# Bias, centring, causal mask and residual moved between TensorE and VectorE, with a new order, in a Mamba and MoE block

## The chip, the cores and the metric

The kernel runs on one core of one Trainium2 chip. The time is the device time of one execution in microseconds. The core has five engines with instruction queues of their own, each in order: TensorE (PE in the profile, with its weight loads as PEld), VectorE (DVE), ScalarE (ACT), GpSimd (POOL) and SyncE (SP), which here only issues DMAs.

## The reference

The input x is 4 x 1024 tokens of 128 numbers, all float32. Two blocks follow each other, each with a residual and a layer norm. First a Mamba block:

```python
xz = x @ in_proj.T; xb, z = split(xz)            # 256 channels each
xb = silu(conv4(xb)); dt = softplus(...); B, C = ...
h[t] = exp(dt*A) * h[t-1] + dt*xb*B              # 16 states a channel
y = (h * C).sum(states) + xb * D_param
y = layernorm(y) * silu(z); x = layernorm(x + y @ out_w.T)
```

Then a transformer block with 16 heads of 8 numbers, causal softmax attention, and a mixture of 16 experts (128 to 512 to 128, gelu), each token going to its best two within a capacity of 512 slots an expert:

```python
q, k, v = layernorm(x) @ q_w, ...                # scores only where key <= query
hidden = x + (softmax(q k / sqrt(8)) v) @ o_w + o_b
xt = layernorm(hidden); top1, top2 = best two of xt @ router_w
out = layernorm(x + hidden + gates * experts(xt))
```

## The kernel before

The tokens are cut into nine units: seven of 512 tokens (0 to 6) and two of 256 (7 and 8, the end of batch 3). A unit passes through these stages, whose names carry its number:

- `conv` and `dt`: the projection, convolution and step sizes, written to DRAM.
- `scan`: the recurrence. A page holds 32 channels x 4 states; VectorE multiplies (`uB`), scans (L527) and multiplies again (`hC`), ScalarE makes the decay (`da`), TensorE sums over the states (`py`).
- `norm`: y is centred by two products with a fixed matrix (`centre`), squared, averaged over channels by 128x1 products (`pvar`), and the inverse root `rs` comes from a power on GpSimd (`inv_power`, L501 on POOL). Then the output projection (`pa`, `pbx`), the residual x by a product with the identity, two layer norms (`affine`), `x1` and `xn`.
- `qk`: queries and keys, each split into three bf16 parts (`part`) that go to DRAM (`parts`) and come back as the operands of the scores.
- `att`: for four groups of four heads, blocks of 128 keys: `scores`, on diagonal blocks a bf16 product of the identity with a mask added into the same bank, the exponential (`pr`) and the average (`av`) on TensorE; at a group's end `avs`, `av_tr`, `rc`, `ctx`.
- `post`: output projection with its bias, which is a product of a row of ones with a row `obp`; layer norm; the row buffer `xrow`, of which there are three, with the token's number copied into its last column by GpSimd (`tokcol`); the router's logits.
- `route`: for chunks of units (0,1), (2,3), (4,5), (6), (7), (8), the two best experts, their slots, and per 128 tokens two indirect sends from `xrow` on GpSimd (L2151).

After them the experts make two passes over 16 experts, the first over slots 0 to 127 and 384 to 511, the second over the middle, each ending in indirect scatters on GpSimd (L2300). `finish` loads the two expert rows of a token (`got`), weights and adds them, on VectorE (L521) or with diagonal matrices on TensorE, normalises and stores.

Nothing of this runs in program order. Each operation is declared with a value `v`, its possible engines and an estimated duration, and a planner (`Plan.schedule`) then simulates the engines: whenever one is free, it takes the ready operation with the lowest `v`. A table `ORDER` adds an offset to `v` by stage and by name of the operation. An operation's `v` is never below that of what it depends on. The planner's result is written out as the fixed order of each engine's queue. The planner does not know the real times: a wrong estimate makes an engine wait in front of an operation that it thinks is ready.

Lines of helpers: L451 matmul, L449 transpose, L479 and L474 ScalarE, L481 to L487 the same work given to VectorE, L501 tensor_tensor, L512 and L514 tensor_scalar, L521 scalar_tensor_tensor, L527 scan, L428 DMAs.

Of the kernel before, what the change touches and what calls it, by code (L numbers as in the profile page):

```python
# [9 lines left out]
F32 = mybir.dt.float32  # L10
# [8 lines left out]
P = 128  # L19
# [41 lines left out]
    "att0": 38, "att1": 41, "att2": 38, "att3": 8.5, "att4": 25, "att5": 9.5, "att6": 22, "att7": 43, "att8": 117,  # L61
    "conv1": 8, "conv2": 22, "conv3": 55, "conv4": -4, "conv6": 8, "conv7": 12, "dt3": 90, "dt5": 43, "fc1": 8,
    "norm0": 45, "norm1": -25, "norm2": -52, "norm3": 5, "norm5": -3, "norm6": -48, "norm7": -26.5, "norm8": 15,
    "place2": 75, "post0": -112, "post1": 3, "post2": 79, "post3": 32, "post4": -87, "post5": 30, "post6": -23,
    "post7": 12, "qk4": 52, "qk6": 22, "qk7": 27, "route0": -107, "route1": -328, "route3": 58, "scan0": 7,
    "scan1": 36, "scan2": 30, "scan3": 26, "scan4": 37.5, "scan5": 22.5, "scan6": 15, "scan7": -1.5, "scan8": 45.5,
    "x1": 160, "av_tr": -308, "avs": -104, "b1_tr": 43, "centre": -78, "constants": -38, "conv": 56.9, "ctx": -74,
    "ctx_tr": 21.5, "dt": 27, "dt_sp": 48, "dtmm": 29, "fin": 72, "first": -9, "flags": 54, "got": 153, "kst": -25,
    "lg": 65, "ln2_ag": 49, "m_t": 49, "part": 7, "pbias": 62, "pqk": 3, "pr": -356, "pv": 16.12, "rc": -135,
    "rest": 132, "rs": 34, "scan": 10, "scores": -2.05, "sz_s": 36, "t_first": 17, "token": 185, "u": 34,  # L70
    "u_sp": 58, "w_out_b": 115, "wide": 71, "x2_tr": 61.5, "xT": 53, "xT0": 49, "x_rows": 39.4, "xe_tr": 4,
    "xnT": 52,
# [115 lines left out]
class Plan:  # L188
    def __init__(self, nc, tc, loaded=None, order=()):
# [57 lines left out]
    def schedule(self):  # L247
# [77 lines left out]
        while n_left:  # L325
# [8 lines left out]
            while again:  # L334
                again = False
                for e in engines:
# [55 lines left out]
                    if op.wire:  # L392
                        bus = max(bus, op.end) + op.wire
                        op.done = bus + (2300 if e == "POOL" else 1500)
# [22 lines left out]
class Emit:  # L417
# [80 lines left out]
    def tt(self, v, out, a, b, op, pool=False, name=""):  # L498
        eng = self.nc.gpsimd if pool else self.nc.vector
        fixed = 250 + 420 * out.cols if op == ALU.pow else None  # L500
# [74 lines left out]
def mamba_then_moe_block_kernel(ctx: ExitStack, tc: tile.TileContext, a: dict, out: bass.AP):  # L575
# [866 lines left out]
    plan_a = Plan(nc, tc)  # L1442
# [193 lines left out]
    def mild_path(ph):  # L1636
        DVE_FROM = 6
# [28 lines left out]
        }  # L1666
        conv_half, dt_half, adopt = fronts_of(p, e, 3)
# [181 lines left out]
        def inv_power(v, pool_name, src, n, two, name):  # L1849
# [3 lines left out]
            if two:  # L1853
                e.ts(v, ve[:, 1, :], src, 1.0 + LN_EPS, LN_EPS * LN_EPS, ALU.mult, ALU.add, name=name)
# [616 lines left out]
```

## Time and profile before

| | |
|---|---|
| median of 6 runs | 1019.6 us (1015.96 to 1024.89) |
| profiled execution | 1019.58 us, span 1017.7 us |
| granted TensorE clock, mean | 0.948 |
| TensorE busy | 872.8 us, 86% |
| VectorE busy | 800.0 us, 79% |
| ScalarE busy | 717.5 us, 71% |
| GpSimd busy | 243.9 us, 24% |
| DMA | 166.14 MB, 163 GB/s on average |

The shares are averages over stages with different limits, so they say little by themselves. The scans end at 735 us; by then unit 7's attention is under way. From there to the end at 1017.7 us come the attention of units 7 and 8, the two expert passes and `finish`. A chain of waits is read backwards from the last instruction: each piece is what released the next.

### The profile page before, as it was taken

The page shows a single profiled execution, that of the slowest core. Times are in us where ns is not written, and L with a number is a line of the kernel's source. Part 1 is how long each engine was busy: PE and PEld are TensorE (multiplying, and loading weights), DVE is VectorE, ACT ScalarE, POOL GpSimd, SP SyncE. Part 2 cuts the span into 40 slices and gives each one's busy share as a digit, 9 for nine tenths or more (in the row PEclk, how much of TensorE's full clock was granted, in tenths as well). Part 3 has the DMA queues.
Part 4 walks back from the last instruction along what each step waited for, and adds up shares of the span by engine and source line. Part 5 has one row for each costly group of instructions (what it writes and reads, how often), then busy time and mean ns, then how long its engine had stood idle before and what let it go on. Part 6 is the DMA issues. An engine that isn't in the chain of part 4 may idle for free.

```text
span 1017.7 us, 17751 instructions
## 1 busy us (share of the span) xinstructions
PE 872.8 (86%) x6309; PEld 471.9 (46%) x6351; DVE 800.0 (79%) x1488; ACT 717.5 (71%) x1152; POOL 243.9 (24%) x340
## 2 busy tenths in 40 slices
PE   7878989779986999998989989988983889997983
PEld 3323344234442345444335443434562448887963
DVE  3999999999999999999989989997952233434234
ACT  3667878649975997997988889886852666453321
POOL 2000000420010001068010110182016133554541
PEclk9999989799988999999998999999996999999997
DMA  4767965887644555575383545263892324215233
GB/s 123 236 222 226 341 230 196 287 251 211 184 126 135 180 148 154 157 227 151 102 263 111 166 116 172 80 186 86 268 259 78 104 69 122 66 58 156 64 115 105
DMA packets 143437, 166.14 MB, mean 163 GB/s; under 512 B 15521, under 2 KB 97764, under 8 KB 143204
## 3 DMA queue, kind: packets, MB, share of 16 engines
q1 hardware_dynamic: 138084, 156.07, 50.4%
q0 software_dynamic: 4096, 8.43, 2.5%
q8 instruction: 54, 0.88, 0.4%
q10 hardware_dynamic: 1152, 0.34, 0.1%
q14 instruction: 51, 0.42, 0.1%
HBM read 108.10 MB, written 56.69 MB: 162 GB/s over the span
## 4 chain that ended last, share of the span: by engine, by line
PE 37%; DVE 25%; DMA 11%; ACT 9%; issue 7%; POOL 6%; another core or an unknown queue 2%; SPq 2%; DVEq 0%; ACTq 0%; POOLq 0%
PE bank L451 21%; PE pair L451 13%; DVE arena L527 11%; DVE arena L501 10%; ACT arena L479 8%; POOL xin L2151 4%; PE bank L449 2%; DMA xin<-rt_full 2%; DVE arena L521 2%; SPq L428 2%; DMA xin<-xrow,rt_put 1%; DMA arena<-q_parts 1%; DMA arena<-eout 1%; DMA arena<-k_parts 1%
## 5 line engine op out<-in xcount | busy, mean ns | idle before, releaser
L479 ACT ACTIVATE arena<-pair 128x1024 f32<-128x1024 f32 (+2 forms) x341 | 302.4, 924 | 58.0 <-PE pair L451 32.7
L501 DVE TENSOR_TENSOR arena<-arena 128x2048 f32<-128x2048 f32 (+2 forms) x154 | 303.1, 1985 | 0.4 <-PE bank L451 0.3
L451 PE MATMUL pair<-arena 128*128 128x256 bf16 (+4 forms) x1079 | 250.0, 329 | 43.3 <-ACT arena L479 22.9
L479 ACT ACTIVATE arena<-arena,f_a_neg 128x512 f32<-128x512 f32 (+1 forms) x284 | 183.7, 680 | 60.1 <-DVE arena L527 48.9
L501 POOL TENSOR_TENSOR smalls<-smalls,neg_half 128x4 f32<-128x4 f32 (+2 forms) x35 | 61.5, 1758 | 514.0 <-DVE smalls L512 351.3
L451 PE MATMUL bank<-arena,vp 128*32 128x256 f32 (+3 forms) x1728 | 166.9, 469 | 3.9 <-ACT arena L474 1.2
L527 DVE TENSOR_TENSOR_SCAN arena<-arena,state 128x512 f32<-128x512 f32 (+1 forms) x160 | 162.1, 1050 | 0.0
L451 PEld LDWEIGHTS <-arena 128*128 128x128 bf16 x864 | 81.0, 99 | 157.1 <-issue 120.9
L527 DVE TENSOR_TENSOR_SCAN arena<-arena 128x512 f32<-128x512 f32 x128 | 150.1, 1204 | 0.0
L2151 POOL DMA_INDIRECT xin<-xrow,rt_put x64 | 88.8, 1388 | 92.2 <-ACT arena L479 30.0
L479 ACT ACTIVATE arena<-pair,b 128x256 f32<-128x256 f32 x128 | 53.6, 471 | 59.7 <-PE pair L451 54.2
L451 PE MATMUL pair<-mask_k,identb 128*128 128x128 bf16 x512 | 94.0, 222 | 1.3 <-issue 0.4
L451 PE MATMUL bank<-arena,f_sel 128*32 128x512 f32 x512 | 71.3, 631 | 19.9 <-DVE arena L501 19.7
L2300 POOL DMA_INDIRECT eout<-arena,to x64 | 62.4, 975 | 55.0 <-DVE arena L501 29.5
L451 PEld LDWEIGHTS bank<-arena,vp 128*32 128x32 f32 x1728 | 38.3, 110 | 63.2 <-issue 42.8
L501 DVE TENSOR_TENSOR arena<-bank,arena 128x256 f32<-128x256 f32 (+2 forms) x46 | 22.0, 479 | 57.7 <-PE bank L451 52.0
L451 PEld LDWEIGHTS bank<-arena 128*128 128x128 f32 x512 | 63.6, 196 | 3.2 <-DVE arena L501 1.2
L451 PE MATMUL bank<-arena 128*128 128x128 f32 x512 | 64.2, 280 | 0.8 <-DVE arena L501 0.8
L451 PEld LDWEIGHTS <-identb 128*128 128x128 bf16 x512 | 50.7, 99 | 9.3 <-issue 7.7
L451 PEld LDWEIGHTS pair<-arena 128*128 128x128 f32 x256 | 44.8, 194 | 13.2 <-ACT arena L479 9.2
L449 PE MATMUL bank<-ident,arena 128*128 128x128 f32 (+1 forms) x257 | 45.3, 289 | 5.3 <-ACT arena L474 2.0
L479 ACT ACTIVATE arena<-arena,smalls 128x128 f32<-128x128 f32 x59 | 26.1, 497 | 30.9 <-DVE smalls L521 30.9
(216 smaller groups left out, 1070.3 us busy)
## 6 DMA issues: line engine op xcount, KB each, us to landing
arena<-k_parts SPq DMA_DIRECT2D x52, 288.0 KB
arena<-bc_h SPq DMA_DIRECT2D x56, 256.0 KB
arena<-dt_h SPq DMA_DIRECT2D x52, 256.0 KB
arena<-u_h SPq DMA_DIRECT2D x52, 256.0 KB
arena<-in_fc_w_dram SPq DMA_DIRECT2D x32, 256.0 KB
q_parts<-halves SPq DMA_DIRECT2D x21, 384.0 KB
k_parts<-halves SPq DMA_DIRECT2D x21, 384.0 KB
arena<-q_parts SPq DMA_DIRECT2D x28, 288.0 KB
```

What stands on the lines that cost most here:

```text
L428: return self.p.add(v, {queue: 460}, lambda e: engine.dma_start(out.real(), in_.real()), [out], [in_], name, wire=wire, after=after)
L449: nc.tensor.transpose(out.real(), lhsT.real(), rhs.real())
L451: nc.tensor.matmul(out.real(), lhsT=lhsT.real(), rhs=rhs.real(), start=bool(start), stop=stop, skip_group_check=start is None)
L479: nc.scalar.activation(out.real(), in_.real(), func, scale=real(scale), **kw)
L501: return self._dve(v, lambda e: eng.tensor_tensor(out.real(), a.real(), b.real(), op), [out], [a, b], out.cols, fixed=fixed, name=name, po ...
L521: return self._dve(v, lambda e: nc.vector.scalar_tensor_tensor(out.real(), a.real(), real(s), b.real(), op0, op1), [out], self._views(a, s ...
L527: return self._dve(v, lambda e: nc.vector.tensor_tensor_scan(out.real(), d0.real(), d1.real(), real(init), ALU.mult, ALU.add), [out], self ...
L2151: inst = nc.gpsimd.indirect_dma_start(out=dst.real()[:, :], out_offset=bass.IndirectOffsetOnAxis(ap=idx.real(), axis=0), in_=src.real(), i ...
L2300: inst = nc.gpsimd.indirect_dma_start(out=eo_d.real()[:, :], out_offset=bass.IndirectOffsetOnAxis(ap=idx.real(), axis=0), in_=src.real(), ...
```

## The change

The functions and constants that change:

- Units 7 and 8 (`u >= MASK_FROM`): no mask product; VectorE multiplies the exponential's diagonal 128x128 blocks of four heads at once by a triangle of ones and zeros (`below`). Their centring is one mean from TensorE (two products) and two additions on VectorE (`apart`).
- The output bias: `obp` is a 128x128 bf16 tile of zeros with the bias, split in three bf16 parts, in rows 0, 32 and 64; it is multiplied by a bf16 tile of ones.
- `pvar`: products with a 128x32 tile into four row groups, a copy `var`, a transpose `pvar_t`.
- Units 6 to 8: the residual x is added by VectorE instead of an identity product.
- `inv_power` and `affine`: the double power is two powers, the second half's first, and so are the products `nm`.
- `tokcol` is placed behind the power and `nm` of its post stage.
- The planner: landing of a GpSimd DMA 3500 ns instead of 2300, a power 80 + 310 ns a column instead of 250 + 420, a send 1450 and a scatter 1320 instead of 1260, loads ahead of the branch 1.5 times as long with a landing of 3000.
- `finish`: blocks 12, 20 and 28 by TensorE instead of 16, 20, 24 and 28.
- Every entry of `ORDER` is new.

```diff
 ORDER = {
-    "att0": 38, "att1": 41, "att2": 38, "att3": 8.5, "att4": 25, "att5": 9.5, "att6": 22, "att7": 43, "att8": 117,
...
+    "att0": -22, "att1": 30, "att2": 43, "att3": 7, "att4": 15, "att5": -0.5, "att6": 29, "att7": 32, "att8": 125,
...
+    "qk1": -175, "qk4": 32, "route1": 37, "route2": -8, "route3": -8, "route5": 49, "scan0": -12, "scan1": -8.5,
+    "scan2": 28, "scan3": 3, "scan4": 10.2, "scan6": -4, "scan7": 21, "scan8": 37.5, "top2": 105, "x1": 154,
+    "x2": 105.5, "av": 23, "av_tr": 26.9, "b1_tr": 4, "before": 45, "below": 90, "bt": 31, "constants": -5,
...
 }
...
-                        bus = max(bus, op.end) + op.wire
-                        op.done = bus + (2300 if e == "POOL" else 1500)
+                        bus = max(bus, op.end) + op.wire * self.wire
+                        op.done = bus + (3500 if e == "POOL" else self.landing)
...
-        fixed = 250 + 420 * out.cols if op == ALU.pow else None
+        fixed = 80 + 310 * out.cols if op == ALU.pow else None
...
-    plan_a = Plan(nc, tc)
+    plan_a = Plan(nc, tc, wire=1.5, landing=3000)
...
-            e.pe(v + 5, [("mm", pb[0:1, 0:D], fx(vbc), fx(wo), True, True)], name="pbias")
-            e.tt(v + 5, fx(obp), ob, pb[0:1, 0:D], ALU.add, name="obp")
+            wide = new("tmp", "vb_wide")[:, 0:P]
+            e.copy(v + 4, wide, fx(vbc).to_broadcast([P, P]), name="obp")
+            e.pe(v + 5, [("mm", pb[:, 0:D], wide, fx(wo), True, True)], name="pbias")
+            e.tt(v + 5, ob, ob, pb[:, 0:D], ALU.add, name="obp")
+            part = wide.bitcast(BF16)[:, 0:D]
+            for i in range(3):
+                e.copy(v + 5, part, ob, name="obp")
+                e.copy(v + 5, fx(obp)[32 * i : 32 * i + 1, :], part[32 * i : 32 * i + 1, :], name="obp")
+                if i < 2:
+                    e.tt(v + 5, ob, ob, part, ALU.subtract, name="obp")
...
-            e.tt(v, r.rearrange("p k n -> p (k n)"), ve.rearrange("p k n -> p (k n)"), fx(neg_half)[:, 0 : k * n], ALU.pow, pool=True, name=name + "_pow")
...
+            for i in reversed(range(k)):
+                e.tt(v, r[:, i, :], ve[:, i, :], fx(neg_half)[:, 0:n], ALU.pow, pool=True, name=name + "_pow")
...
+            if u >= MASK_FROM:
+                mean = new("bank", "centred")[:, 0:n]
+                e.pe(v, [("mm", mean, fx(center)[:, 1, :], y[c], c == 0, c == NC2 - 1) for c in range(NC2)], name="centre")
             for c in range(NC2):
-                pt = new("bank", "centred")[:, 0:n]
-                e.pe(v, [("mm", pt, fx(center)[:, 0, :], y[c], True, False), ("mm", pt, fx(center)[:, 1, :], y[1 - c], False, True)], name="centre")
+                if u >= MASK_FROM:
+                    pt = new("tmp", "apart")[:, 0:n]
+                    e.tt(v + 0.5, pt, y[c], mean, ALU.add, name="apart")
+                else:
...
-            e.pe(v + 2, [("mm", pv[:, i : i + 1], sqs[c][:, tok(i)], fx(mean_col), c == 0, c == NC2 - 1) for i in range(nt) for c in range(NC2)], name="pvar")
+            pv = new("bank", "pvar")[:, 0:P]
+            e.pe(v + 2, [("mm", pv[32 * i : 32 * i + 32, :], fx(mean_w), sqs[c][:, tok(i)], c == 0, c == NC2 - 1) for c in range(NC2) for i in range(nt)], share=3.4, name="pvar")
+            var = new("var")[:, 0:P]
+            e.act(v + 2, var[0 : 32 * nt, :], pv[0 : 32 * nt, :], AF.Copy, dve=u >= DVE_FROM, name="var")
+            pv = new("bank", "pvar_t")[:, 0:P]
+            e.pe(v + 2, [("tr", pv[:, 0 : 32 * nt], var[0 : 32 * nt, :], fx(ident)[0 : 32 * nt, 0 : 32 * nt], 0, 0)], name="pvar_t")
+            pv = pv[:, 0 : 32 * nt : 32]
...
+            if u >= DVE_FROM:
+                e.tt(v + 4.5, xp, xp, r, ALU.add, name="xp")
...
-                            if diag:
+                            if masked:
                                 calls.append(("mm", pst[:, jj, :P], fx(identb), fx(mask_k), False, True))
...
+                        if diag and u >= MASK_FROM:
+                            e.tt(vv + 0.1 * j0 + dv * 0.6, pr[:, 0:per, 0:P], pr[:, 0:per, 0:P], fx(tri).unsqueeze(1).to_broadcast([P, per, P]), ALU.mult, name="below")
...
-            e.copy(v, xrow[:, :, D], fx(token)[:, tile0 : tile0 + nt], pool=True, name="tokcol")
+            p.behind(e.copy(v, xrow[:, :, D], fx(token)[:, tile0 : tile0 + nt], pool=True, name="tokcol"), [rr_op])
...
-        by_pe = range(2 * TPB, NT, 4)
+        by_pe = (12, 20, 28)
```

## The prediction

> **What bounds the kernel now.** I read the slices of the span first, to see which engine is full when; then a table of stages that I cut at the places where that changes; then the chain of waits inside the two stages where nothing is full; then the groups, for prices. Busy tenths of three engines in 40 slices of 25.4 us:
>
> ```profile
> PE   7878989779986999998989989988983889997983
> DVE  3999999999999999999989989997952233434234
> PEclk9999989799988999999998999999996999999997
> ```
>
> VectorE is full for some 28 slices, then TensorE for the rest, with a hole at slices 30 and 31. The stages (PE, weight loads, VectorE, ScalarE, GpSimd in us, then granted clock, DMA share, GB/s):
>
> ```profile
> 50.00:735.00 685.00, 603.63 (x4302) 277.14 (x4345) 662.98 (x887) 560.56 (x864) 121.11 (x96) 0.96 0.59 184
> 768.00:788.00 20.00, 5.36 (x40) 2.24 (x39) 0.95 (x8) 2.71 (x6) 14.73 (x29) 0.62 0.31 94
> 788.00:843.00 55.00, 48.12 (x531) 27.27 (x532) 14.91 (x104) 37.01 (x46) 13.31 (x25) 0.95 0.30 86
> 932.00:938.00 6.00, 0.71 (x5) 0.40 (x4) 3.01 (x15) 1.15 (x4) 5.26 (x9) 0.90 0.22 67
> 938.00:982.00 44.00, 44.00 (x279) 39.80 (x280) 11.42 (x33) 17.58 (x43) 26.75 (x50) 0.94 0.21 63
> 982.00:1017.70 35.70, 14.35 (x131) 10.80 (x129) 17.50 (x89) 4.41 (x11) 6.46 (x7) 0.77 0.49 140
> ```
>
> To 735 us VectorE (scans) has 22.0 us idle in 685. After that nothing new comes from the scans, and TensorE should run through; it does not in 768 to 788 (14.6 us idle) and 932 to 938 (5.3 us idle). What the chain says there, and at 687 to 696 where ScalarE starved (start, us, what):
>
> ```profile
> 686.60 5.14 DMA xin<-xrow,rt_put
> 691.89 1.29 POOL xrow L540
> 693.18 2.75 POOL smalls L501
> 695.95 0.63 ACT arena L479 x2
> ...
> 767.62 3.58 another core or an unknown queue
> 772.52 5.16 another core or an unknown queue
> 778.18 4.45 another core or an unknown queue
> 782.75 5.66 another core or an unknown queue
> ```
>
> The first is a queue effect: GpSimd's token copy waits 4.07 us for a send that still reads its buffer, and the power that unit 7's `rs` needs stands behind it. The second has no named releaser. In it GpSimd alone works, on the 16 sends of units 4 and 5, one every 1.26 us from 765.4, while ScalarE moves unit 8's query and key parts in steps of about 5 us. Prices (the last column before the bar is the count, after it busy us and mean ns):
>
> ```profile
> L451 PE MATMUL pair<-mask_k,identb 128*128 128x128 bf16 x512 | 94.0, 222 | 1.3 <-issue 0.4
> L501 DVE TENSOR_TENSOR arena<-arena 128x512 f32<-128x512 f32 x23 | 15.4, 675 | 0.1
> L451 PE MATMUL bank<-obp,ones_row 1*128 1x512 f32 x14 | 7.8, 640 | 0.1
> L501 POOL TENSOR_TENSOR smalls<-smalls,neg_half 128x8 f32<-128x8 f32 x7 | 17.5, 2504 | 100.7 <-DVE smalls L514 79.6 <-DVE smalls L512 21.1
> L501 POOL TENSOR_TENSOR smalls<-smalls,neg_half 128x4 f32<-128x4 f32 x24 | 39.1, 1628 | 394.6 <-DVE smalls L512 311.9 <-DVE rt_full L501 40.7 <-DVE flags L512 30.3
> ```
>
> **The sum's base** is the profiled execution: 1019.6 us, of which 1017.7 is span; the median of the runs is the same 1019.6.
>
> **The change part by part.** *Mask.* 64 of the 512 mask products go (units 7 and 8: 4 groups x 2 diagonal blocks x 4 heads each). They are pipelined: at 826 us a score and its mask take 0.17 us from start to start, a score alone 0.11, so each saves 0.055, 3.5 us of TensorE. VectorE gets 16 multiplies of 128x512, 16 x 0.68 = 10.8 us, in 768 to 843, where it is a quarter busy. Each stands between the exponential and the average, whose next scores are already out; uncovered only at a group's end, 8 x 0.7 = 5.6 us. Queued behind a multiply that waits for its exponential are VectorE's copies of finished averages and the routing of units 6 and 7; VectorE's 40 free us of 55 there take that up. Between -3.5 and +2; I take -3, since TensorE has other scores to run.
>
> *Bias.* The f32 row product (1.12 us a pair) becomes one bf16 product; the 128x512 bf16 row with neg_identb takes 0.39. 0.7 us a unit; only units 6 to 8 lie behind the scans: -1 (0 to -2). The new constants are some nine small VectorE instructions of 0.23 (the cast of a 128x128 at 21 us): +2, inside VectorE's full stage. The bias is now loaded into 128 rows, 64 KB instead of 512 bytes, still one issue on SP's queue in the first 60 us; the 128 KB load of `center` beside it is of the same kind: 0.
>
> *Centring, units 7 and 8.* TensorE loses half of 2.08 us for both; VectorE gains 4 x 0.42 (128x256 from PSUM), 0.84 of it in the full stage. *Residual, units 6 to 8.* TensorE loses 1.2 + 0.6 + 0.6; VectorE gains 0.68 + 2 x 0.42, of it 1.1 in the full stage; TensorE's part after 735 counts -1.
>
> *Variance.* Sixteen short products (1.0 us) become sixteen in four row groups (0.43 for eight, as the averages with vp), a copy (0.37 ScalarE, 0.27 VectorE) and a transpose (0.31). TensorE gains nothing to speak of, the chain to `rs` gets 0.7 longer. VectorE's other work hides it in units 0 to 7; unit 8: +0.7.
>
> *Powers.* One 128x8 of 2.50 us becomes two 128x4 of 1.63, the wanted one first: `xn` starts 0.9 earlier, `x1` 0.8 later, GpSimd works 0.76 more a unit. Hidden by the scans, in units 7 and 8 about -0.5. The doubled `nm` adds 0.15 to VectorE in seven units before 735: +1.
>
> *Token copy* goes behind the post stage's power. The 4.07 wait no longer holds `rs`; what is late next is ScalarE's turn on the exponentials: -3 (0 to -4).
>
> VectorE's full stage thus grows by 2 + 0.84 + 1.1 + 1 = 5 us; its 22 idle could swallow it (0), but full slices lie close together, so +5.
>
> *Last sums.* One more block of eight on VectorE (8 x 0.28 = 2.2), one less on TensorE (about 2.4 by 16 x 0.15). Both wait for the same loads: -1 (-3 to +2).
>
> *Order.* All offsets are new, so are a send's landing (3500 for 2300) and the price of a power and a send, and the planner moves everything: loads on SP's queue, sends and powers on GpSimd's. Which instruction stands where I can't read from the offsets. From below its gain ends at the idle time: 14.6 + 5.3 + 22.0, about 42 us. From above it can make as big a hole as the 20 us of 768 to 788 a second time. I take 10 of the first hole, as sends are now held to land later so that work behind them is planned apart, 3 of the second (the scatters and the first `got` loads are also re-placed) and nothing of VectorE's: -13. The first branch's own new prices for loads touch the 50 us before the scans fill VectorE: 0 (-3 to +3).
>
> Sum: -3 -1 -1 +0.7 -0.5 -3 +5 -1 -13 = -16.8, so 1003.
>
> **A rule against it.** Row: unit 7's 128x2 power at 693.1 took 2.78 us while VectorE ran two 128x2048 multiplies for 4.48; the twice as wide power at 935.6, with VectorE nearly idle, took 1.04. The Trainium skill, SBUF — State Buffer, Who interferes with whom, says that a VectorE instruction with two SBUF inputs locks out a GpSimd one that reads SBUF, for its whole length. The new multiplies are of that kind. By the rule each could hold up a power or send, 16 x 0.68 = 11 us of GpSimd at worst, and the sum would be near 1014. The sum above sets 0: GpSimd has 42 us free in 788 to 843.
>
> **Rivals.** *(a) The hole closes.* If 768 to 788 is only the meeting of 16 sends with unit 8's parts, another order ends it: all 14.6 and 5.3 go, and 5 of VectorE's idle: local terms -3.8, order -25: 991. For it: GpSimd is the only busy engine there. Against: no releaser is named, so the order may not reach it.
>
> *(b) The order moves nothing.* Only the local terms remain: 1019.6 - 3.8 = 1016. For it: VectorE and TensorE are at 97% and near 100% in their stages. Against: two holes and a starved power that are queue effects.
>
> *(c) Slower.* GpSimd's sends come in front of unit 8's power. Place: after the scans' end, 735 to 768, where unit 8 runs centre to query product in 28 us with GpSimd 5.7 busy in 33. If 16 sends of 1.26 stand ahead of its two powers, its attention starts up to 20 later; the old hole can't hide this, for then TensorE has only unit 7. It decides from seven sends on: 8.8 us less the local 3.8 is the 5 that can be told. Price 20 - 4 = +16: 1035; with half, 1026. For it: the sends come in batches of 16 already, and routing's place moves by tens of units. Against: a send's price is raised, which pulls powers ahead.
>
> **How the numbers follow.** Forecast 0.40, (a) 0.24, (b) 0.14, (c) 0.22. What can be told from no change is 0.5%, 5 us. Faster: forecast, (a) and a fifth of (b), 0.67; same: the rest of (b), 0.11; slower: (c), 0.22. The range: (a) with 12 more of VectorE's idle used, 979, to half of (c) and its spread, 1030. The forecast with (a) alone would span 979 to 1014.
>
> **What would show it.** mask_k rows 448 instead of 512, sixteen more 128x512 VectorE products, no 128x8 power, an obp product in bf16, and no token copy between a landing send and a power. The stage of full VectorE should end at 735 to 742. The forecast is wrong if TensorE still idles over 10 us in one piece after 760, if the hole has moved rather than closed, or if VectorE's stage ends after 750.

## The result, and the profile after

The changed kernel takes 1028.88 us (median of 20 runs, 1020.72 to 1034.78) where the kernel before takes 1018.25 in runs beside it (46 runs, 1013.4 to 1027.13). The ratio on record, which is not the quotient of the two medians (that would be 1.0104), is 1.0086, with a 95% interval of 1.0065 to 1.0107: slower by 0.86%. The forecast was 1003, with 979 to 1030 as its range. The profiled execution took 1026.14 us, with a span of 1024.3 and a mean granted clock of 0.947 (before: 1019.58, 1017.7, 0.948).

The slices of the changed kernel, busy tenths in 40 slices of 25.6 us:

```profile
PE   8868879877996999999969889897986899997983
DVE  2999999999999999999889999997971445334124
PEclk9989999997999999999989999998997899999996
```

VectorE's 30th slice is busy for 7 tenths instead of 5, and the hole of TensorE behind it is still there, in slice 31. The stages, with the first cut moved to where the scans now end (columns as in the prediction). "The scans end" means here, and in all that follows, the end of the last product that sums over the states on TensorE (`py`); the last scan instruction on VectorE ends 3.5 to 4.0 us before it:

```profile
50.00:742.50 692.50, 600.52 (x4446) 265.79 (x4489) 664.99 (x904) 572.08 (x888) 116.02 (x107) 0.96 0.58 179
768.00:788.00 20.00, 9.87 (x67) 4.34 (x66) 1.93 (x4) 4.05 (x6) 12.49 (x24) 0.76 0.33 88
788.00:843.00 55.00, 47.99 (x498) 25.46 (x500) 23.79 (x138) 36.07 (x45) 13.59 (x25) 0.93 0.35 99
932.00:938.00 6.00, 2.06 (x5) 1.71 (x6) 2.71 (x15) 1.58 (x4) 4.33 (x7) 0.82 0.21 66
982.00:1024.30 42.30, 21.83 (x158) 14.78 (x156) 17.99 (x94) 7.71 (x19) 10.24 (x13) 0.72 0.43 123
```

The place of the loss can be read without any experiment. The scans end at 734.8 us before and at 742.5 after, 7.7 later; from there to the end of the span it is 282.9 before and 281.8 after. The repeats below scatter more: two profiles of before end their scans at 734.8 and 734.6 us and need 282.9 and 278.4 from there; four of the changed kernel end them at 742.5, 743.8, 744.1 and 741.3 and need 281.8, 280.0, 282.5 and 282.0. On average that is 8.2 later at the end of the scans, and 0.9 longer behind it. So nearly all of the loss is there when the scans end, inside the stage that VectorE bounds, and behind it nothing was gained. In that stage VectorE is busy 662.9 us before and 665.0 after (+2.1), and idle 21.9 before and 27.5 after (+5.6): what grew is mainly waiting. The view of VectorE's waits in that stage (us in total, times, longest) says for which work. Before:

```profile
DVE smalls L536 <- PE bank L449: 6.9, 3, 3.3
...
DVE arena L501 <- ACT arena L479: 4.6, 4, 2.4
...
DVE smalls L521 <- POOL smalls L501: 0.9, 2, 0.6
```

After:

```profile
DVE smalls L521 <- POOL smalls L501: 8.3, 3, 7.0
DVE arena L521 <- issue: 6.1, 1, 6.1
...
DVE smalls L536 <- PE bank L449: 0.9, 2, 0.7
DVE arena L501 <- ACT arena L479: 0.6, 1, 0.6
```

The new order took 10.0 us of these two kinds of small waits away (6.9 to 0.9, and 4.6 to 0.6) and put two long ones in: 7.0 us of a wait for a GpSimd power, and a stop of 6.1 us for which the profile names nothing ("issue"). The rest of the +5.6 is a net of smaller waits. In the three repeats of the changed kernel and in one more kernel with the same order the first is 7.0 us three times and 5.7 once, the second 5.5 (with ScalarE named as the releaser) to 6.3. The chain of waits of the changed kernel (start, us, what) passes through both, and through the old hole:

```profile
505.66 4.90 POOL xin L2185
...
515.63 1.08 POOL smalls L501
...
702.41 6.08 issue
...
777.35 8.51 another core or an unknown queue x2
```

The first of them in the timeline (start, us, and in brackets the idle time before). GpSimd:

```profile
505.66 4.90 POOL L2185 DMA_INDIRECT xin<-xrow,rt_put  x1 [0.22 <-issue]
...
510.86 0.96 POOL L2185 DMA_INDIRECT xin<-xrow,rt_put  x1 [0.22 <-issue]
...
514.65 0.95 POOL L2185 DMA_INDIRECT xin<-xrow,rt_put  x1 [0.22 <-issue]
515.63 1.07 POOL L501 TENSOR_TENSOR smalls<-smalls,neg_half 128x4 f32<-128x4 f32 x1
```

VectorE in the same microseconds:

```profile
505.24 4.48 DVE L501 TENSOR_TENSOR arena<-arena 128x2048 f32<-128x2048 f32 x2
516.73 0.16 DVE L521 SCALAR_TENSOR_TENSOR smalls<-smalls 128x4 f32<-128x4 f32 x1 [7.00 <-POOL smalls L501]
...
516.99 1.27 DVE L527 TENSOR_TENSOR_SCAN arena<-arena,state 128x512 f32<-128x512 f32 x1
```

GpSimd's queue has the 16 sends of units 0 and 1 in one batch, from 484.1 to 515.6 us, and behind them the power of a layer norm. VectorE's `nm` (L521), which needs it, stands in VectorE's queue ahead of a scan, which starts 0.26 us after it. VectorE, which bounds this stage, waits 7.0 us with work behind it. The batch takes 31.5 us, where 16 sends at the 1.26 us that the trace of before shows would be 20, because a send beside large multiplies is stretched (4.90 against 0.96). The batch and its length are not what is new: the kernel before sends the same 16 from 438.6 to 477.5 us, and has a power behind them, at 480.3. There VectorE's longest wait for a power in the whole stage is 0.6 us.

The counts are as the change says. From the groups by form of the changed kernel (count, then busy us and mean ns, then idle before):

```profile
L451 PE MATMUL pair<-mask_k,identb 128*128 128x128 bf16 x448 | 83.9, 222 | 1.1 <-issue 0.2
L501 DVE TENSOR_TENSOR arena<-arena,tri 128x512 f32<-128x512 f32 x16 | 10.7, 686 | 17.8 <-ACT arena L479 17.7
L451 PE MATMUL bank<-obp,some_b 128*128 128x512 bf16 x7 | 2.7, 381 | 0.9 <-DVE arena L501 0.9
```

There is no 128x8 power any more, and no token copy between a landing send and a power that `rs` needs.

### The profile page after: what moved, and what is told of

It reads as the page before. It is cut to its first block, busy times and chain, and to the rows that moved or that the text cites. A ratio compares the mean times of both kernels' runs of the same rounds, so it can differ in the third digit from the quotient of the medians.

```text
span 1024.3 us, 18030 instructions
## 1 busy us (share of the span) xinstructions
PE 874.1 (85%) x6419; PEld 456.8 (45%) x6463; DVE 806.2 (79%) x1513; ACT 731.2 (71%) x1179; POOL 238.4 (23%) x350
## 4 chain that ended last, share of the span: by engine, by line
PE 31%; DVE 18%; ACT 6%; DMA 5%; issue 5%; POOL 3%; another core or an unknown queue 1%; SPq 0%; ACTq 0%; DVEq 0%; POOLq 0%
PE bank L451 16%; PE pair L451 13%; DVE arena L527 7%; DVE arena L501 7%; ACT arena L479 6%; POOL xin L2185 2%; DMA arena<-q_parts 2%; PE bank L449 2%; DMA arena<-eout 1%; DVE arena L521 1%; DMA arena<-k_parts 1%; DVE smalls L566 1%; POOL smalls L501 1%; DMA arena<-in_fc_w_dram 1%
## 5 line engine op out<-in xcount | busy, mean ns | idle before, releaser
L451 PE MATMUL pair<-arena 128*128 128x256 bf16 (+4 forms) x1077 | 247.0, 332 | 45.6 <-ACT arena L479 33.0
L501 POOL TENSOR_TENSOR smalls<-smalls,neg_half 128x4 f32<-128x4 f32 (+1 forms) x44 | 59.7, 1363 | 500.0 <-DVE smalls L512 467.8
L2185 POOL DMA_INDIRECT xin<-xrow,rt_put x64 | 82.3, 1286 | 70.3 <-issue 30.7
L451 PE MATMUL bank<-arena,f_sel 128*32 128x512 f32 x512 | 74.0, 652 | 18.5 <-DVE arena L501 17.6
L451 PE MATMUL pair<-mask_k,identb 128*128 128x128 bf16 x448 | 83.9, 222 | 1.1 <-issue 0.2
L451 PEld LDWEIGHTS <-identb 128*128 128x128 bf16 x448 | 44.4, 99 | 15.8 <-issue 14.1
L1438 PE MATMUL bank<-some_b,zero_b 128*32 128x512 bf16 (+1 forms) x660 | 50.0, 420 | 1.1 <-DVE bnd_s L544 1.1
```

The source lines that it names most:

```text
L451: nc.tensor.matmul(out.real(), lhsT=lhsT.real(), rhs=rhs.real(), start=bool(start), stop=stop, skip_group_check=start is None)
L501: return self._dve(v, lambda e: eng.tensor_tensor(out.real(), a.real(), b.real(), op), [out], [a, b], out.cols, fixed=fixed, name=name, po ...
L1438: nc.tensor.matmul(to[32 * j : 32 * j + 32, :], lhsT=zero_b, rhs=some, start=view is None, stop=view is None)
L2185: inst = nc.gpsimd.indirect_dma_start(out=dst.real()[:, :], out_offset=bass.IndirectOffsetOnAxis(ap=idx.real(), axis=0), in_=src.real(), i ...
```

## The experiments

They were run on several chips, and one fact of these is needed to read them: on some chips (the first kind, two in these runs) the kernel before takes 1016 to 1018 us, on others (the second kind, two) 992 to 994. Each ratio compares kernels on one chip. The repeats of the changed kernel, all on chips of the first kind, gave 1.0106, 1.0113 and 1.0113 (expectations below); in their traces the scans end at 741.3 to 744.1 us, in that of the kernel before again at 734.6. So the later end is no accident of one trace.

> The kernel before, unchanged, for a profile on the same chip as the kernels run with it. In the first comparison of the two kernels the chip took 1018 us for it, the chip of the four mixtures 992 us. Theory S (on some chips the whole core stops between 766 and 789 us while GpSimd sends rows, whatever the order): the profile shows the stop of some 20 us exactly when the time is near 1018, and none when it is near 992. If the stop belongs to the order alone, it is there at both times.

Measured: 1014.91 us in a single run, beside a median of 1016.32 of the same program.

> The changed kernel, unchanged, on this chip. If the loss lies in the longer stage of full VectorE (scans' end 742.5 us against 734.8), 1.006 to 1.011 on any chip, and the scans end 5 to 9 us later than in the kernel before on this chip. If it lies in the stop, the ratio moves with it: below 1.004 on a chip that does not show it.

Measured: 1027.46, ratio 1.0106 [1.0068, 1.0143].

> The changed kernel, unchanged, beside the two below on one chip. Where the kernel before takes about 1016 us (its profile has the stop at 766 to 789 us): 1.007 to 1.011, as twice before. Where it takes about 993 us (no stop): theory Q (VectorE's 7.0 us behind GpSimd's sends at 512 to 519 us is in the order and stays, the 6 us of 702 to 708 belong to the chip): 1.001 to 1.006. If the whole loss belongs to the stops: 0.996 to 1.001. If to neither: 1.008 or more.

Measured: 1028.80, ratio 1.0113 [1.0084, 1.0142].

> The changed kernel, unchanged, beside the one above. Where before takes about 1017 us: 1.008 to 1.012 again. Where it takes about 993 us, theory Q says 1.001 to 1.006 (7 us behind the sends of units 0 and 1, no stop at 702 to 708 us, and the gains of the change); 1.008 or more would mean that the loss does not depend on the stop.

Measured: 1026.12, ratio 1.0113 [1.0073, 1.0154].

### Order and edits apart

The edits of the change with the order, the planner's prices and the last sums of before:

```diff
 ORDER = {
-    "att0": -22, "att1": 30, ...
+    "att0": 38, "att1": 41, ...
...
-    plan_a = Plan(nc, tc, wire=1.5, landing=3000)
+    plan_a = Plan(nc, tc)
...
-        by_pe = (12, 20, 28)
+        by_pe = range(2 * TPB, NT, 4)
```

> All of the change's edits to the arithmetic, with the order table, the planner's prices and the VectorE share of the last sums (by_pe) of the kernel before. Theory L (the edits cost the time themselves: more VectorE work in 50-735 us and dearer small steps): as slow as the changed kernel, 1.007 to 1.011 times before. Theory O (the new order and prices cost it, the edits are worth what the prediction's terms other than the order say, -3 to -4 us): 0.995 to 0.998, with the whole-core stall near 768 us still there. Rival C (order and edits belong together, any mixture is worse than either pure kernel): over 1.012.

Measured: 1028.86 beside 992.26, ratio 1.0346 [1.0311, 1.0382].

The other mixture: the kernel before with the new order, prices and last sums, the same lines the other way round.

> The kernel before with the changed kernel's order table, planner prices and by_pe, and none of its other edits. Theory L: 0.985 to 1.001, since the new order is then no loss. Theory O: 1.008 to 1.013, the whole loss without any edit. Rival C: over 1.012 here and over 1.012 in the other mixture too; the two together then tell O from C, since O asks for the other mixture below 1.

Measured: 1024.19 beside 992.26, ratio 1.0285 [1.025, 1.032]. Its scans end at 754.8 us, those of the first mixture at 749.6. In the second mixture VectorE waits for powers even longer than in the changed kernel (waits, 50 to 754 us):

```profile
DVE arena L501 <- PE bank L451: 13.1, 13, 4.6
DVE smalls L521 <- POOL smalls L501: 12.4, 4, 5.5
```

Each mixture is 3% slower than before, the last of the three outcomes named for them. An order of this kind seems to belong to one set of operations and durations; neither mixture gives the value of a half, and the question "edits or order" can't be answered by swapping them. It has to be asked of single waits.

How much a planner's order moves by a trifle was tried on the kernel before, with one offset changed by one:

```diff
-    "scan": 10,
+    "scan": 11,
```

> The kernel before with one number of its order table moved by one (scan 10 to 11), nothing else; the planner then moves a large part of all instructions. It measures what any new plan of the same work is worth. Theory P (the given table was fitted, any neighbour is worse): 1.005 to 1.03, as large as the whole loss of the change. If the plan matters little: within 0.5% of before, and the 2.9 and 3.5% of the mixtures came from something particular in them.

Measured: 1013.27 beside 1016.32, ratio 0.9972 [0.9939, 1.0005], though, counted place by place, 4027 of TensorE's 6309 recorded instructions are of another kind than in the kernel before. So a new order need not cost 0.9%; it is one neighbour only. Its scans end at 727.0 us, 7.6 to 7.8 earlier than those of before, and the time hardly follows: TensorE works 3.27 us from 760 to 782. An order can thus move the end of the scans by as much as the whole loss, and what lies behind can take it back.

### Single edits

The last sums alone (`by_pe`). In the changed kernel the old choice, and in the kernel before the new one:

```diff
-        by_pe = range(2 * TPB, NT, 4)
+        by_pe = (12, 20, 28)
```

> The changed kernel with four blocks of the last sums on TensorE again (16, 20, 24, 28) in place of three (12, 20, 28). Theory F (the 5 us by which the time from the last expert's second product to the end grew, 37.3 to 42.3 us, comes from the VectorE share of the last sums): 1.003 to 1.005 times before, that is 4 to 6 us below the changed kernel. If the three blocks are right for this order: 1.008 to 1.011, no gain. The plan of everything ahead of the last stage may move too, by an unknown amount; the end's own stretch, from the last second product on, tells it apart.

Measured: 998.82 beside 992.26, ratio 1.0055 [1.0028, 1.0081]. The changed kernel itself was not timed on a chip of this kind, so this says nothing of the last sums; but it is the nearest to a time of the change there, and more than half of the 0.86% is in it. VectorE's waits to the end of its scans, at 738.9 us, have the power and no stop:

```profile
DVE smalls L521 <- POOL smalls L501: 11.4, 4, 7.0
DVE rt_full L512 <- DMA xin<-rt_full: 3.7, 3, 1.9
```

> The kernel before with the last sums as in the changed one (blocks 12, 20, 28 by TensorE, the others by VectorE). Theory F: 1.004 to 1.006, with 41 to 43 us from the last second product to the end in place of 37.3. If the end is set by something else (the last rows coming back, the order of the final normalization): within 0.2% of before.

Measured: 999.33 beside 992.26, ratio 1.0038 [1.0008, 1.0069]. So in the kernel before, one more block of eight on VectorE costs 1 to 7 us. In the traces the stretch from the end of the last scatter to the end of the span is 35.4 and 36.3 us in two profiles of before, 38.3 in this one, 36.3 to 37.9 in four profiles of the changed kernel, and 36.2 in the changed kernel with the old choice.

The mask. The changed kernel with its 16 multiplies left out, everything else at its place:

```diff
-... ALU.mult, name="below")
+... ALU.mult, name="below").emit = lambda eng: None
```

> The changed kernel without the sixteen VectorE multiplies that mask the exponentials of the last two units (the mask is left out there: nothing takes their place). The order of all other instructions is exactly that of the changed kernel. What VectorE's part of the mask costs on the path: the prediction says nearly nothing (VectorE is a quarter busy there): within 2 us of the changed kernel. If each multiply holds up the averages behind it: 16 x 0.68 = 10.9 us at most, so 4 to 11 us below the changed kernel. By the page's rule on VectorE and GpSimd, sends would also end earlier by up to 11 us.

Measured: 1027.56, beside 1027.46 of the changed kernel on the same chip (ratios 1.0102 and 1.0106, each known to 0.4%). The 10.7 us of VectorE's multiplies cost nothing on the path that can be told.

The token copy. In the kernel before, the two copies after the sends of units 2 and 3 go behind the power that follows:

```diff
+            sends = [o for o in order if o.stage == "route1" and (o.name == "first" or o.name.startswith("second"))]
...
+            late = [o for o in rest[:rest.index(power)] if o.name == "tokcol"]
+            order = [o for o in order if o not in late]
+            at = order.index(power) + 1
+            order[at:at] = late
```

> The kernel before with GpSimd's two token copies that follow the sends of units 2 and 3 moved behind the power that follows them; all else in the same order. It is the change's soft order of the token copy alone. The prediction's term: the wait of 4.07 us and the copy's 1.3 go from the path of the last unit but one, 3 to 4 us less (0.996 to 0.997). If VectorE's stage does not wait for that unit (it has other scans), or ScalarE is late next: within 0.1%.

Measured: 1015.03, ratio 0.9971 [0.994, 1.0002]: a gain of 3 us can't be told from none. The timeline says why the whole 3 can't be expected there:

```profile
691.11 4.90 POOL L514 TENSOR_TENSOR smalls<-smalls,neg_half 128x2 f32<-128x2 f32 x1 [0.81 <-DVE smalls L525]
```

The power's own input comes only at 691.1, and the power, now beside two whole large multiplies, takes 4.90 us. It ends at 696.0, as it did behind the token copies (at 693.14, 2.78 long, it ended at 695.9). What was late next was the power itself.

### The power behind the sends

The theory: the 7.0 us at 510 to 517 are the queue's doing, and an order with that one power ahead of the last sends takes them away. Rival: VectorE would wait there for something else, and the time stays. The changed kernel, with one GpSimd power moved ahead of the last five sends of units 0 and 1, all other instructions in their order:

```diff
+            sends = [o for o in order if o.stage == "route0" and (o.name == "first" or o.name.startswith("second"))]
+            if sends:
+                power = next(o for o in order[order.index(sends[-1]):] if o.name.endswith("_pow"))
+                order = [o for o in order if o not in sends[-5:]]
+                at = order.index(power) + 1
+                order[at:at] = sends[-5:]
```

> The changed kernel with one power of GpSimd moved ahead of the last five sends of units 0 and 1, all other instructions in the same order on every engine. Theory Q: the wait of VectorE for it falls from 7.0 us to 1 to 3 us (one send may still be in work, and one took 4.9 us beside two multiplies of VectorE), the scans end 4 to 6 us earlier, and the time is 4 to 6 us below the changed kernel (0.4 to 0.6%). If VectorE's stage has other waits that take its place: within 2 us.

Measured: 1020.47, ratio 1.0047 [1.0025, 1.0069], beside 1028.80 of the changed kernel on the same chip (1.0113): 8.3 us less by the medians, 6.7 by the ratios, from one power's place. Its timeline, GpSimd:

```profile
507.54 5.22 POOL L512 TENSOR_TENSOR smalls<-smalls,neg_half 128x4 f32<-128x4 f32 x1
...
512.99 1.04 POOL L2196 DMA_INDIRECT xin<-xrow,rt_put  x1 [0.17 <-issue]
```

VectorE:

```profile
507.36 4.48 DVE L512 TENSOR_TENSOR arena<-arena 128x2048 f32<-128x2048 f32 x2
512.79 0.17 DVE L532 SCALAR_TENSOR_TENSOR smalls<-smalls 128x4 f32<-128x4 f32 x1 [0.94 <-POOL smalls L512]
```

The wait falls from 7.00 to 0.94. VectorE's and ScalarE's instructions, matched one by one with those of the changed kernel on the same chip, start within 0.2 us of each other from 360 to 520 us, 7.0 earlier from 520 on, and 5.3 to 7.3 earlier up to the last scatter. The scans end at 738.0, there at 744.1. The power itself is no faster there: beside the two multiplies it takes 5.22 us, where it took 1.07 with VectorE idle. It is only early enough.

### The stop, and the hole

What is left is the stop of 6.1 us at 702 to 708, and the question what the old hole is. In both, nothing that the profile names is late, and GpSimd alone goes on, with sends, while the other three do little: from 702 to 708 us of the changed kernel TensorE works 2.23 us, VectorE 0.41 and ScalarE 1.02, and in the hole of before 5.36, 0.95 and 2.71 of 20. The theory (S in the expectations): the sends bring the stop. Rival: the order of unit 8's parts makes it. The kernel before with the 32 sends of units 2 to 5 left out:

```diff
                             def emit(q):
+                                if c in (1, 2): return
                                 nc.gpsimd.memset(spacer, 0.0)
                                 inst = nc.gpsimd.indirect_dma_start(
```

> The kernel before without the 32 sends of units 2 to 5 (their rows are not written; the plan of everything else is unchanged). Theory S (a run of GpSimd's sends stops the other engines in steps of about 5 us): where the kernel before takes about 1016 us, 15 to 22 us less (0.978 to 0.985), and no wait without a releaser between 760 and 790 us. If the order, the attention loads or SP's queue make the hole of 768 to 788 us, as the prediction had it: within 0.4% of before. On a chip where the kernel before takes 992 us: within 0.4%.

Measured on a chip of the second kind: 1002.44 beside 993.92, ratio 1.007 [1.0031, 1.0109].

> The changed kernel without the same 32 sends. Theory S: 20 to 27 us less than the changed kernel (0.984 to 0.991 of before), of it 4 to 6 us ahead of the end of the scans, since its sends of units 2 and 3 stop the scans at 702 to 708 us. The two kernels without sends then differ by the rest of the loss: 2 to 5 us, the VectorE work that was added ahead of 735 us, against 8 us of later scans' end as they are. If the scans' later end has nothing to do with sends, they still differ by 8 to 11 us.

Measured on the same chip: 997.97, ratio 1.0054 [1.0024, 1.0084]. Neither gains. The reason is in the windows: on chips of this kind there is no hole to take away. The kernel of the first of these was therefore run again on a chip of the first kind:

> The kernel before without the sends of units 2 to 5, once more, in case this chip shows the stop. Where before takes about 1016 us: 15 to 22 us less if the sends make the stop, within 0.5% of before if not. Where before takes about 993 us it can't tell, and should repeat 1.003 to 1.011.

Measured: 1001.09 beside 1017.94, ratio 0.983 [0.9791, 0.9869]. The stretch from 760 to 812 us (PE, weight loads, VectorE, ScalarE, GpSimd, clock, DMA share, GB/s), of the kernel before, on a chip of the first kind:

```profile
760.00:812.00 52.00, 33.50 (x320) 19.07 (x319) 13.88 (x101) 23.99 (x33) 21.98 (x43) 0.80 0.34 97
```

Without the 32 sends, on a chip of the first kind:

```profile
760.00:812.00 52.00, 49.20 (x512) 28.16 (x511) 21.91 (x169) 35.42 (x47) 9.34 (x18) 0.93 0.37 102
```

The kernel before but for `by_pe`, with all its sends, on a chip of the second kind:

```profile
760.00:812.00 52.00, 49.99 (x568) 29.96 (x567) 23.92 (x181) 40.18 (x53) 28.03 (x54) 1.00 0.46 128
```

The changed kernel, on a chip of the first kind:

```profile
760.00:812.00 52.00, 34.70 (x306) 18.46 (x299) 18.33 (x102) 21.15 (x30) 26.63 (x50) 0.84 0.49 136
```

The changed kernel but for `by_pe`, on a chip of the second kind:

```profile
760.00:812.00 52.00, 47.54 (x541) 27.11 (x541) 27.47 (x147) 39.27 (x50) 30.61 (x58) 1.00 0.56 158
```

TensorE works 33.5 and 34.7 of 52 us where sends run on a chip of the first kind, and 47.5 to 50.1 where the sends, or that kind of chip, or both are missing. So the hole is neither order's: the same order, but for the last sums, has it on one chip and not on another, and it goes with the sends. Without these 32 sends the program takes 1002.44 us on a chip of the second kind and 1001.09 on one of the first, so the 24 us between the kinds of chip go with them. How a send stops the other engines, and why only on some chips, no run shows. Sends alone are not enough: on a chip of the first kind the kernel before makes the same 16 sends of units 2 and 3 at 659 to 688 us, and VectorE works 33.3 of the 35 us from 655 to 690. One rival was not tested, that the engines lack instructions, which are loaded by DMA (queues q8 and q14). Their packets take 0.49 to 1.57 us each from 755 to 795 us in the kernel before, and 0.31 to 1.33 in `e4_before_bype_new` on a chip without the hole, so they are hardly slower; whether they came too late can't be read.

A time without sends needs one correction. From the end of the last output store's issue on SyncE's queue to the end of the span it is 7.8 to 9.2 us in the 16 traces with all sends, but 14.0 to 15.8 in the four that leave sends out; in the trace, GpSimd's closing drain takes 7.9 us there with 32 sends left out and 9.2 with 16, instead of 1.87, and the program waits for it. With the stretch of the parent kernel in its place (8.6 for before, 8.8 for the changed one), the three above would be near 995.5 (15.5 - 8.6 less), 992.0 (14.8 - 8.8 less) and 995.7 (14.0 - 8.6 less); ratios of 1.002, 0.998 and 0.978. These are worked out, not measured.

Whether the sends' density makes the stop was to be seen by 12 more one-element writes ahead of each send of units 4 and 5, in both kernels:

```diff
-                                nc.gpsimd.memset(spacer, 0.0)
+                                [nc.gpsimd.memset(spacer, 0.0) for _ in range(13 if c in (2,) else 1)]
```

> The kernel before with twelve more GpSimd fills of one element ahead of each send of units 4 and 5 (0.09 us each, 1.1 us a send), so that one goes every 2.4 us and not every 1.26; nothing else moves in the order. If it is their density that stops the core: 5 to 20 us less than before (0.98 to 0.995). If each send has its price whatever lies between: no gain, and up to 16 x 1.1 = 18 us lost where the next powers and sends of GpSimd come late (1.0 to 1.018).

Measured: 1022.55 beside 993.92, ratio 1.0254 [1.0199, 1.0308].

> The changed kernel with the same twelve fills ahead of each send of units 4 and 5. Density: 5 to 18 us less than the changed kernel (0.993 to 1.005 of before). A price for each send: 1.01 to 1.025.

Measured: 1023.11, ratio 1.0293 [1.0238, 1.0347]. They ran on a chip without the stop, so the question of density stays open. Both lose more than the most that was expected (1.018 and 1.025). They show two other things, though. Up to the end of the scans nothing was touched in them, so they compare the two kernels there on a chip without the stop: the scans end at 735.3 us in the first and at 741.8 in the second, whose longest wait of VectorE is again 7.0 us for a power, with no stop in its list. In the pair of the last sums above, on such a chip too, the ends are 737.3 (order of before) and 738.9. So the change ends its scans 1.6 and 6.5 us later there, where it is 8.2 on the others; in the pair without the sends of units 2 to 5 (737.0 and 734.9) it ends them earlier, though a wait of 5.7 us for a power is still in it. The second thing is in the waits of the first between 785 and 822 us:

```profile
DVE smalls L521 <- POOL spacer L2150: 29.3, 1, 29.3
```

The releaser that is named is a write ahead of a send, but in GpSimd's queue unit 8's power comes next, at 817.5 us, behind sends of which 16 now come one every 3 us. The kernel loses about what it waits, 29 us by the medians and 25 by the ratio: this is the prediction's rival (c) at about its own place.

Last, the two together: the power moved ahead as above, and the 16 sends of units 2 and 3, beside which the stop of 702 to 708 stands, left out. The theory that sends bring the stop expects that the rest of the loss goes.

```diff
+                                if c in (1,): return
```

> The changed kernel with the power ahead of the five sends, and without the 16 sends of units 2 and 3 (rows not written). It takes both waits from VectorE's stage. Where before takes about 1017 us: 12 to 14 us below the changed kernel, 0.996 to 1.000 of before, the scans' end back at 731 to 735 us; that would account for the whole loss by two runs of sends. If the stop moves to other places of the stage: 1.002 to 1.006, as with the power alone. Where before takes about 993 us: the sends cost little there, 0.993 to 1.000.

Measured: 1024.31 beside 1016.30, ratio 1.0096 [1.0058, 1.0134]. By the plain time the theory fails, and the expected 0.996 to 1.000 is missed; by the trace it holds. VectorE's waits to the end of the scans, at 729.9 us:

```profile
DVE rt_full L523 <- DMA xin<-rt_full: 3.6, 4, 1.3
...
DVE smalls L532 <- POOL smalls L512: 2.2, 3, 0.9
```

With the sends of units 2 and 3 in place and the power moved, to 738.0 us:

```profile
DVE arena L532 <- issue: 6.1, 1, 6.1
...
DVE smalls L532 <- POOL smalls L512: 2.2, 3, 0.9
```

The stop is gone and the scans end 8.1 us earlier, of which 6.1 are the stop. The two ran on different chips of the first kind, but are level to 0.6 us from 520 to 680 us; from 720 on everything is 6 to 8 us earlier up to the end of the scatters. The issue of the last store ends 15.8 us before the end of the span, in the kernel with the power moved alone 8.4. With 8.4 here too the time would be 1024.31 - 7.4 = 1016.9, a ratio of 1.0006 by the medians and 1.0023 from the ratio on record: no loss left that could be told. That the second half of the loss is the stop is therefore shown in the trace and, as a time, only worked out.

## Why the prediction was wrong

The sign was wrong; the measured time lies within the range, near its upper end, and that is luck: the range reached there for rival (c) at another place. By place, the sum had +2 up to the end of the scans (+5, and -3 for the token copy) and -18.8 behind it. Measured, on average of the profiles, are +8.2 and +0.9. So the larger miss is the gain behind the scans that did not come, 13 of it the order's, and the smaller one the loss inside them.

**The order term, -13, is the step that failed.** It took 10 of the 14.6 idle us of 768 to 788 and 3 of 932 to 938 as the gain of a new order, since they looked like queue effects. The first is none that an order alone decides: the order of before has it on chips of one kind and lacks it, but for the last sums, on the other, and in the changed kernel TensorE's idle time of 760 to 812 us is 17.3, after 18.5. In 932 to 938 it is 3.9, after 5.3. What the order did do stands in the stage that the term set at nothing: it put a batch of sends ahead of a power that VectorE needs soon (+7.0 in the trace; moving that power gave 6.7 to 8.3 back), it put the sends of units 2 and 3 where their stop hits VectorE in its full stage (about +6 in the trace), and it removed 10.0 us of small waits.

**Rival (c) had the mechanism, at another place.** "GpSimd's sends come in front of unit 8's power", in 735 to 768, at +16: the sends came in front of a power, but in the scans, at 485 to 517. It was confined to the time after the scans by the thought that earlier VectorE's other work hides a late power. It does not where the instruction that waits stands in VectorE's queue ahead of the scans. The chance of 0.22 for it went to one place, where the change moves every batch.

**VectorE's stage, +5 to its end, less 3 for the token copy:** predicted to end at 735 to 742, measured 742.5, and 741.3 to 744.1 in the repeats. The number nearly held by luck, for another reason: its busy time grew by 2.1, not 5, and its idle time by 5.6. The 22 idle us that "could swallow it" were a net of waits removed and waits put in.

**Mask, -3, and the other terms behind the scans:** that VectorE's side of the mask costs nothing holds as far as can be told (16 multiplies of 0.686 us, 0.04% apart with and without them). What the 64 products less gave TensorE, and what bias, centring, residual, variance and powers are worth, was not measured alone. From the end of the scans to the end of the last scatter the two profiles of before take 247.6 and 242.1 us and four of the changed kernel 243.7 to 244.9, so all terms of that stretch together show no gain: mask, bias, residual, variance and powers were put at -4.8 and the holes at -13. In the two kernels without 32 sends, on a chip without the hole, the stretch is 221.8 before and 215.4 after; the local terms may be in that, but it is one trace of each.

**Bias:** the row product was put at 0.39 and takes 0.381. **Token copy, -3:** not to be told from 0; it was forgotten that the power's input is late too and that the power would then run beside VectorE's multiplies. **Last sums, -1:** the wrong sign. In the kernel before they cost +1 to +7; in that stretch the traces have 37.2 us on average in the changed kernel and 35.9 in that of before.

**The rule that was weighed** (the Trainium skill, SBUF — State Buffer, Who interferes with whom) holds for the power: 5.22 us beside two VectorE multiplies with two SBUF inputs, 1.07 without. It was weighed at the mask's multiplies, where it cost nothing, and not in the scan stage, where such multiplies are the rule and the batch of sends runs. The prediction let the rule hold up a send as well. The same page infers the opposite, that such a multiply leaves the making of DMA descriptors alone, and these rows do not fit that inference: a send that began at 505.66 beside multiplies that ended at 509.72 took 4.90 us, and one at 693.41 beside a multiply that ended at 695.54 took 2.96; each ends 0.83 to 0.84 us after the multiply, where a send alone takes 0.96. The measurement decides for these indirect sends; whether it is their descriptors or the row numbers, which lie in SBUF, that wait, no run shows.

**The signs named beforehand:** TensorE idled 10.1 of the 20 us from 768 to 788, but in pieces and not in one (9.87 busy), VectorE's stage did not end after 750, and mask count, bias and powers were as told. The sign that would have caught the loss, VectorE waiting for a power inside the scan stage, was not on the list.

## What to carry to other kernels

When an order is rewritten, look first at the engine that is full: ask for each of its in-order instructions that needs a slow queue (here a power on GpSimd) what stands ahead of its producer, and put the batches of long instructions behind it. An idle stretch for which the profile names no releaser is not a gain that an order can be counted on to collect; run the same program on another chip first. Swapping whole orders between versions says little; moving one instruction, with all else in place, settled 7 to 8 us.

## What the runs showed of the hardware that was not expected

- Beside a batch of GpSimd's indirect sends (one every 1.26 us), VectorE and ScalarE stand still for 4.7 us and more at a time with no named releaser (VectorE 6.1 at 702, ScalarE 4.7 there and 8.5 at 777 in the changed kernel, VectorE 19.6 in the hole of before), and TensorE does little, on some chips and not on others: 1017 against 993 us for the same program, and 1001.09 against 1002.44 without 32 of the sends. The cause is open, and whether wider spacing helps too.
- A send is held up by VectorE's multiplies of two SBUF inputs like a power: 4.90 us instead of 0.96, and it ends 0.83 to 0.84 us after the multiply.
- With 16 or 32 of the 128 indirect DMAs left out, GpSimd's closing drain takes 7.9 to 9.2 us instead of 1.87, and the program ends later by it. An experiment that leaves DMAs out should look at the end of its trace before its time is read.

No complete version was shown to be faster than both kernels.
